# Handing out the first FFN and the preparation of a batch one unit later, and loading x from ScalarE's queue

## Chip, core and metric

The kernel runs on one core of a Trainium2 chip. The metric is the device time of one launch in microseconds, as the median of several runs. A profiled execution of the same program gives the trace and the page from which the lines below come.

The names of the engines are those of the profile: PE is TensorE (matmuls, transposes), PEld its weight loads, DVE is VectorE, ACT is ScalarE, POOL is GpSimd, and SP is SyncE, which does no arithmetic and issues most DMAs. Each engine works through its own instructions in order. An instruction that waits for a semaphore, a DMA issue too, holds everything that stands behind it on its engine.

## What is computed

x has 16 batches of 512 tokens with 128 features. Two layers follow each other. Layer 0, the only one that the change touches, is this:

```python
x = x + 0.5 * _L0_ffn_ref(_layernorm(x), w_gate, w_up, w_down)
x = x + _L0_attn_ref(_layernorm(x), W_qkv, b_qkv, W_out, b_out, rel_emb_k, rel_emb_v)
x = x + 0.5 * _L0_ffn_ref(_layernorm(x), w_gate, w_up, w_down)
```

The FFN quantizes its input, its weights and its hidden values to FP4 in blocks of 16 (`fp4_quant_dequant`) and computes `silu(gate) * up` with 352 hidden values. The attention has 16 heads of 8 features and relative positions, clipped at 64, in both the scores and the values; the softmax runs over all 512 keys of a batch. Layer 1 has another FFN with attention, routing to 8 experts and two layer norms, a linear attention with running sums, and the first part once more.

## The kernel before

Layer 0 is written as steps that Python generators hand out. A **unit** is half a batch: unit u = 2b + h is half h of batch b, so there are 32. The steps of a batch b are:

- `xload(b)` takes one of five buffers of the pool `xk` for the batch's x (128x4x128) and loads it through SP's queue (L475).
- `head(b,h)` runs the first FFN on half h, in place, through `FFN.half` (L107 to L140): layer norm statistics on DVE (L55, L56), normalisation on ACT (L62), quantization on DVE and POOL (L70 to L81), matmuls with a tanh on ACT (L121 to L126), a second quantization, transposes and the last matmul (L133 to L139), and the sum into x on DVE (L140). Its first step calls `xload`.
- `prep(b)` is `Attn0.prep` (L275): layer norm, transposes, q and k, each split into two f16 parts (cast L143 on DVE, difference L144 on POOL). q also goes into the tiles HM (L298). Then DMAs write to DRAM: twelve to QM (L300), three to QS and three to KSd (L302), and four rows to QS (L309). The small parts of these rows are made on DVE (L307, `qkhi` and `qklo`). `qklo` has one buffer, so that each writing of it waits until the DMA that reads the one before is done.
- `loads(u)` reads these back in the order the matmuls need: KS (L315, once per batch), BD (L329) and TQ (L330). KSd, QS and QM have two buffers by batch, BD and TQ three by unit.
- `maxima(u)` computes all 32 score blocks of a unit on PE (L263, and L267 for the relative positions) and takes their maxima on DVE (L341). At its end the negative maxima (`mn`, L352) go to DRAM as MD (L353) and come back as a row of BD (L355), so that the next scores already have the maximum taken off.
- `main(u)` computes the scores again, ACT takes exponentials into PT (L369), and PE multiplies them with the values into `av` and with the relative values into `rps`. `rps` is copied to RV (L403), goes to DRAM as RD (L406) and comes back turned as `cr` (L409); `av` is copied to `cx` (L412).
- `fin(u)` adds the two (L422), divides, multiplies with the output weights and adds to x (L442, L443).
- `tail(u)` runs the second FFN on the half and stores it (L486). When both halves of a batch are stored, its x buffer is free for a batch five later.
- `prepV(b)` makes the values V from the transposed x (L321).

The score tiles `sps` share three PSUM banks between `maxima` and `main`, and all other small results (`mps`) share two.

`interleave` decides in which order the steps are handed out. Every entry has a generator, its number of steps n, and a time from f to t in units; the entry whose next step is due first, at f + (t - f) * done / n, is handed out next. `at(g,n,f,t)` adds u to both times. This order is the priority for the framework's scheduler, which then writes each engine's instructions in the order in which it finds them ready. Before, the due times of a unit u = 2b + h are:

```python
pl,hl=2,3
W=dict(part=0,V=(.6,.7),fin=(.45,.9),prep=(0,.7),tail=1.0,head=(-.1,1))
```

So in unit 2b the preparation of batch b + 2 is due from 0 to 0.7, and in units 2b and 2b + 1 the two halves of the first FFN of batch b + 3, each from -0.1 to 1. The maxima run as one long stream, a unit and a half ahead of `main`; half a unit's maxima into unit u, the loads of u + 1 are handed out. Ahead of the loop stand batches 0 to 2 of the first FFN and the preparation of batches 0 and 1.

Of the kernel before, what the change touches and what calls it, by code (L numbers as in the profile page):

```python
# [141 lines left out]
def f16split(nc, src, hi, lo, eng_lo):  # L142
    nc.vector.tensor_copy(hi,src)  # L143
    eng_lo.tensor_tensor(lo,src,hi,ALU.subtract)  # L144

class Attn0:

    def __init__(a, s, wk, pp, wqkv, bqkv, wout, bout, rek, rev):
# [27 lines left out]
        OFF=a.OFF=168  # L176
        W=EW+32
        ekt=wk.tile([8,129],F32,name="ekt")
        with nc.allow_non_contiguous_dma(reason="small"):
            nc.sync.dma_start(ekt,rek.rearrange("r d -> d r"))  # L180
        nc.vector.tensor_tensor(ekt[:,1:],ekt[:,1:],ekt[:,0:1].to_broadcast([8,128]),ALU.subtract)
        pad=wk.tile([8,W],F32,name="pad")
        lo=OFF+24-64
        nc.vector.memset(pad[:,0:lo+1],0.0)
        nc.vector.tensor_copy(pad[:,lo+1:lo+129],ekt[:,1:129])
        nc.vector.tensor_copy(pad[:,lo+129:],ekt[:,128:129].to_broadcast([8,W-lo-129]))
        ph=wk.tile([8,W],F16,name="ph"); pl=wk.tile([8,W],F16,name="pl")
        f16split(nc,pad,ph,pl,nc.vector)
        padk=dr.tile([24,W],F16,name="padk")
        nc.sync.dma_start(padk[0:8],ph); nc.sync.dma_start(padk[8:16],ph); nc.sync.dma_start(padk[16:24],pl)  # L190
# [255 lines left out]
def interleave(*gens):  # L446

    live=[[g,n,0,f,t] for g,n,f,t in (q if len(q)==4 else (*q,0,1) for q in gens)]
    while live:
        k=min(live,key=lambda r:r[3]+(r[4]-r[3])*r[2]/r[1])  # L450
        try: next(k[0]); k[2]+=1
        except StopIteration: live.remove(k)
# [4 lines left out]
def layer0(tc, s, w, src, dst, nb=16):  # L457
    nc=tc.nc
    tok=lambda x,b: x[b].rearrange("(t p) d -> p t d",p=128)
    P="L0_attn_"; names=["W_qkv","b_qkv","W_out","b_out","rel_emb_k","rel_emb_v"]  # L460
    with ExitStack() as c:
        s.const=c.enter_context(tc.tile_pool(name="c",bufs=1))
        pM=c.enter_context(tc.tile_pool(name="pM",bufs=2,space=PS))
        pF=c.enter_context(tc.tile_pool(name="pF",bufs=0,space=PS)) if 0 else pM
        pS=c.enter_context(tc.tile_pool(name="pS",bufs=3,space=PS))
        pX=pS
        pA=c.enter_context(tc.tile_pool(name="pA",bufs=1,space=PS))
        wk=c.enter_context(tc.tile_pool(name="wk",bufs=1))
        fk=c.enter_context(tc.tile_pool(name="fk",bufs=2))
        xk=c.enter_context(tc.tile_pool(name="xk",bufs=5))  # L470
        X={}
        def xload(b):
            if b in X or b>=nb: return
            t=xk.tile([128,4,128],F32,name="x"); X[b]=t
            nc.sync.dma_start(t,tok(src,b))  # L475
        def head(b,h):

            if b<nb: xload(b); yield from F.half(X[b],h,fk,pF)
        def prep(b):
            if b<nb: yield from A.prep(b,X[b],wk,pM)  # L480
        def prepV(b):
            if b<nb: yield from A.prepV(b,pM)
        def tail(b,h):
            if b<0: return
            yield from F.half(X[b],h,fk,pF)
            nc.sync.dma_start(tok(dst,b)[:,2*h:2*h+2,:],X[b][:,2*h:2*h+2,:])  # L486
        def mxs(b,half):
            if b>=nb: return
            yield from A.maxima(b,half,wk,pX,pM)
        def loads(u):  # L490
            if u<2*nb:
                if u%2==0: A.loadK(u//2)
                A.load(u//2,u%2)
        def stream():
            for u in range(1,2*nb):
                for k,_ in enumerate(mxs(u//2,u%2)):
                    if k==16: loads(u+1)
                    yield
        st=stream()
        def part(n):  # L500
            for _ in range(n):
                if next(st,0)==0: return
                yield
        pl,hl=2,3
        W=dict(part=0,V=(.6,.7),fin=(.45,.9),prep=(0,.7),tail=1.0,head=(-.1,1))
        with tc.tile_pool(name="wp",bufs=1) as wp:
            for b in range(3): xload(b)
            F=FFN(s,w["L0_ffn_w_gate"],w["L0_ffn_w_up"],w["L0_ffn_w_down"],wp,pF)
            ffn2=lambda f,b: interleave((f(b,0),21,0,.8),(f(b,1),21,.2,1))
            ffn2(head,0)  # L510
            A=Attn0(s,wp,pS,*[w[P+n] for n in names])
            def run(g):
                for _ in g: pass
            run(prep(0)); run(prepV(0)); loads(0); run(mxs(0,0))
            FFN1.pre(s,wp,[pA.tile([128,512],F32,name=f"av{z}") for z in range(2)]+[pA.tile([128,512],F32,name="rps")],w)
        big=c.enter_context(tc.tile_pool(name="big",bufs=3))
        loads(1); ffn2(head,1); run(prep(1)); run(part(14)); ffn2(head,2)
        S=[(part(99999),33*2*nb,W['part'],2*nb+W['part'])]
        for b in range(nb):
            for h in range(2):  # L520
                u=2*b+h
                def at(g,n,f,t): S.append((g,n,u+f,u+t))
                at(A.main(b,h,X,wk,big,pS,pA,pM),59,0,1)
                fn,tl=(W['fin'],W['tail']) if u<2*nb-2 else ((.3,.5),.6)
                at(A.fin(b,h,X,wk,pM),5,1+fn[0],1+fn[1])
                at(tail(b,h),21,1+fn[1]+.001,1+fn[1]+tl)
                if b+hl<nb: at(head(b+hl,h),21,*W['head'])
                if h==0 and b+pl<nb: at(prep(b+pl),11,*W['prep'])
                if h==1 and b+1<nb: at(prepV(b+1),1,*W['V'])
        interleave(*S)  # L530
# [251 lines left out]
class Attn1:  # L782
# [38 lines left out]
    X={}  # L821
# [188 lines left out]
def run_stages(ctx, tc, w, out):  # L1010
    s = K(ctx, tc)
    X2 = s.dram.tile([16, 512, 128], F32, name="X2")
    layer0(tc, s, w, w["L0_attn_x"], X2)
    layer1(tc, s, w, X2, out)
# [23 lines left out]
```

## Time and profile before

| what | value |
|---|---|
| median of 3 runs | 3630.38 us (3630.13 to 3631.83) |
| the profiled execution's own time | 3633.94 us |
| its span, first to last instruction | 3632.2 us |
| mean granted TensorE clock | 0.900 of full speed |
| first exponential of unit 0, and of unit 1 | 175.5 us, 237.4 us |
| last exponential of unit 31 ends | 1975.1 us |

A span's busy shares are means over stages that differ: layer 0 takes the first 2045 us or so, layer 1 the rest. Rows of the profile give the line, the engine, the operation, what it writes and reads, how often, and microseconds. A row of waits reads: engine and line, `<-` what released it, microseconds in total, times, longest. Rows of a timeline begin with the start and the duration in microseconds and end, in brackets, with the idle time of the engine before them and what ended it.

### The profile page before, as it was taken

What the parts mean: (1) busy time and instruction counts of PE and PEld (TensorE: products, weight loads), DVE (VectorE), ACT (ScalarE), POOL (GpSimd) and SP (SyncE); (2) the same over time, 40 slices, a digit from 0 to 9 for tenths busy, and PEclk for the clock granted to TensorE, in tenths of its full rate; (3) what the DMA queues carried; (4) which work ended last, traced back from release to release, by engine and by line L of the source; (5) the groups of instructions that cost most, each with busy time, mean ns of one, the idle gap of its engine ahead of it and who ended that gap; (6) DMA issues with size and microseconds to landing.
All of it is one profiled execution on the core that took longest, in us unless ns stands there. A gap on an engine that the chain in (4) does not pass through costs nothing. (4 is left out here: it accounts for less than half of the span.)

```text
span 3632.2 us, 95259 instructions
## 1 busy us (share of the span) xinstructions
PE 2825.0 (78%) x40077; PEld 2032.3 (56%) x40077; DVE 2444.9 (67%) x6508; ACT 1693.8 (47%) x3391; POOL 838.9 (23%) x789
## 2 busy tenths in 40 slices
PE   5578989889898889888896388873788888878570
PEld 3357777667676677666775244431565555555230
DVE  5568788777887788877773467774546655655356
ACT  3145555545455454545554155533455454445242
POOL 4122222222222222222110222212112211111226
PEclk8799999999999999999998599886899989989785
DMA  3232222321223222222210111104312222121401
GB/s 105 54 91 71 57 53 59 81 63 52 65 65 77 64 50 58 76 74 62 53 33 19 32 33 36 36 33 123 90 54 73 59 63 56 36 62 36 126 17 46
DMA packets 290159, 217.23 MB, mean 60 GB/s; under 512 B 77402, under 2 KB 257476, under 8 KB 289604
## 3 DMA queue, kind: packets, MB, share of 16 engines
q1 hardware_dynamic: 284468, 207.72, 21.6%
q8 instruction: 315, 5.16, 0.6%
q10 hardware_dynamic: 5264, 3.43, 0.4%
q14 instruction: 112, 0.92, 0.1%
HBM read 110.28 MB, written 100.78 MB: 58 GB/s over the span
## 5 line engine op out<-in xcount | busy, mean ns | idle before, releaser
L341 DVE TRANSPOSE_TENSOR_REDUCE mx<-sps 128x16 f32<-128x512 f32 x1024 | 702.5, 701 | 261.7 <-PE sps L263 137.2
L263 PE MATMUL sps<-a_BD,a_KS 128*128 128x128 f16 x8192 | 736.4, 222 | 136.2 <-DVE mx L341 65.6
L369 ACT ACTIVATE PT<-sps 128x512 f32<-128x512 f32 x1024 | 576.4, 599 | 433.8 <-PE sps L267 238.1
L263 PEld LDWEIGHTS <-a_KS 128*128 128x128 f16 x8192 | 546.1, 98 | 296.4 <-issue 260.0
L59 POOL TENSOR_TENSOR ln_rs<-ln_ve,negh 128x4 f32<-128x4 f32 (+1 forms) x192 | 176.9, 930 | 855.1 <-DVE ln_ve L58 760.6
L267 PE MATMUL sps<-a_TQ,a_ET 128*128 128x64 f16 x7168 | 370.3, 195 | 0.0
L721 DVE SCALAR_TENSOR_TENSOR moe<-mps,oh,moe 128x128 f32<-128x128 f32 x896 | 289.8, 341 | 110.7 <-PE mps L719 96.5
L79 POOL TENSOR_TENSOR q_M<-q_y,q_M 128x704 f32<-128x704 f32 (+2 forms) x129 | 157.0, 1218 | 784.6 <-DVE q_y L78 658.6
L719 PE MATMUL mps<-f_W,T 128*128 128x512 f32 x512 | 297.1, 701 | 24.8 <-DVE moe L721 20.0
L267 PEld LDWEIGHTS <-a_ET 128*128 128x128 f16 x7168 | 311.2, 99 | 2.3 <-issue 1.9
L274 PE MATMUL av<-PT,a_V 128*32 128x256 f32 x3840 | 251.9, 387 | 0.0
L894 DVE TENSOR_TENSOR a_at<-pp,a_cm 128x1024 f32<-128x1024 f32 x128 | 154.3, 1214 | 79.6 <-PE pp L892 78.6
L892 PE MATMUL pp<-a_F 64*128 64x128 f32 x2048 | 169.8, 306 | 41.4 <-DVE a_at L894 30.2
L892 PEld LDWEIGHTS pp<-a_F 64*128 64x128 f32 x2048 | 143.3, 206 | 93.0 <-DVE a_at L894 36.9
L719 PEld LDWEIGHTS mps<-f_W,T 128*128 128x128 f32 x512 | 102.7, 222 | 125.0 <-issue 75.3
L274 PEld LDWEIGHTS av<-PT,a_V 128*32 128x32 f32 x3840 | 121.4, 111 | 68.7 <-issue 5.0
L874 ACT ACTIVATE a_F<-pp 128x1024 f32<-128x1024 f32 x128 | 127.0, 1025 | 46.8 <-PE pp L872 40.5
L62 ACT ACTIVATE xn<-xn,ln_mr,ln_rs 128x128 f32<-128x128 f32 x256 | 103.6, 481 | 95.5 <-DVE ln_mr L60 75.2
L274 PE MATMUL rps<-PT,a_TV 128*32 128x64 f32 x6912 | 134.5, 222 | 4.6 <-issue 4.4
L139 PE MATMUL mps<-wdT,hT 128*128 128x128 f32 (+1 forms) x768 | 126.9, 301 | 5.6 <-ACT hT L136 4.0
L673 ACT COPY f_PT<-St 32x512 f32<-32x512 f32 x128 | 78.7, 615 | 106.0 <-DVE St L672 99.9
L872 PE MATMUL pp<-a_QK,a_PK 128*128 128x512 f16 x256 | 82.7, 413 | 54.4 <-DMA a_QK<-a1d 26.6
(342 smaller groups left out, 5330.2 us busy)
## 6 DMA issues: line engine op xcount, KB each, us to landing
QM<-a_HM SPq DMA_DIRECT2D x180, 128.0 KB
a_TQ<-QM SPq DMA_DIRECT2D x120, 192.0 KB
RD<-RV SPq DMA_DIRECT2D x32, 512.0 KB
a_KS<-KSd SPq DMA_DIRECT2D x128, 96.0 KB
a_QK<-a1d SPq DMA_DIRECT2D x128, 96.0 KB
xn<-X SPq DMA_DIRECT2D x32, 256.0 KB
a1d<-a_hi SPq DMA_DIRECT2D x64, 128.0 KB
a_BD<-QS SPq DMA_DIRECT2D x128, 58.0 KB
```

What stands on the lines that cost most here:

```text
L59: nc.gpsimd.tensor_tensor(rs,ve,s.negh[:,:n],ALU.pow); yield
L79: nc.gpsimd.tensor_tensor(M[:P],y[:P],M[:P],ALU.subtract)
L263: nc.tensor.matmul(o4[:,g],KS[:,sd,g*512+kt*128:g*512+(kt+1)*128],BD[:,g,:,b*32:b*32+32].rearrange("p h (x j) -> p x h j",j=4),start=(g==0 ...
L267: nc.tensor.matmul(out[:,x*64:x*64+64],a.ET[:,w0:w0+128],TQ[:,:,b*32+4*x:b*32+4*x+4],start=False,stop=(x==7),skip_group_check=True)
L274: for p,q in mms[1:]: a.nc.tensor.matmul(*p,**q)
L341: with a.s.tc.high_priority(): r=nc.vector.tensor_reduce(mx[:,kt,:,bb],ps.rearrange("p (i c) -> p i c",c=32),axis=AX.X,op=ALU.max,apply_tr ...
L369: nc.scalar.activation(pt[:,:,bb*32:bb*32+32].rearrange("p h (x j) -> p x h j",j=4),ps.rearrange("p (x h j) -> p x h j",x=8,j=4),AF.Exp)
L719: nc.tensor.matmul(ps,yT[:,j*128:(j+1)*128],a.W[:,e2*4:e2*4+4,:],start=True,stop=True)
L721: nc.vector.scalar_tensor_tensor(moe[:,j,:],ps[:,e*128:(e+1)*128],oh[:,j,e2*4+e:e2*4+e+1],moe[:,j,:],ALU.mult,ALU.add)
L874: nc.scalar.activation(f,ps,AF.Relu)
L892: nc.tensor.matmul(ps[:,hh,bs],f[hh*64:hh*64+64,1,bs],f[hh*64:hh*64+64,0,bs],start=True,stop=True)
L894: nc.vector.tensor_tensor(k,ps.rearrange("p h (b q) -> p (h b) q",b=4),a.cm.unsqueeze(1).to_broadcast([128,8,128]),ALU.mult)
```

## The change

Three things change in `layer0`; no arithmetic is added or taken away.

- `head` no longer loads x. A step of its own, `xl(b)`, loads it through ACT's queue (`nc.scalar`); it is due in unit 2b of two batches before at -1.4 to -1.3. Batches 0 to 2 are still loaded ahead of everything through SP.
- The first FFN of batch b + 2 (no longer b + 3) is due from -1.05 to 0 of units 2b and 2b + 1. For one batch this is a unit later. As hl is now 2, batch 2 is handed out inside the loop; due times are kept from falling below 0.
- The preparation of batch b + 2 is due from 1.03 to 1.9 of unit 2b, that is in the odd unit that follows.

```diff
-        def xload(b):
-            if b in X or b>=nb: return
+        def xload(b, eng=nc.sync):
             t=xk.tile([128,4,128],F32,name="x"); X[b]=t
-            nc.sync.dma_start(t,tok(src,b))
+            eng.dma_start(t,tok(src,b))
+        def xl(b):
+            xload(b,nc.scalar); yield
         def head(b,h):
 
-            if b<nb: xload(b); yield from F.half(X[b],h,fk,pF)
+            if b<nb: yield from F.half(X[b],h,fk,pF)
...
-        pl,hl=2,3
-        W=dict(part=0,V=(.6,.7),fin=(.45,.9),prep=(0,.7),tail=1.0,head=(-.1,1))
+        pl,hl=2,2
+        W=dict(part=0,V=(.6,.7),fin=(.45,.9),prep=(1.03,1.9),tail=1.0,head=(-1.05,0))
...
-        loads(1); ffn2(head,1); run(prep(1)); run(part(14)); ffn2(head,2)
+        loads(1); ffn2(head,1); run(prep(1)); run(part(14))
...
-                def at(g,n,f,t): S.append((g,n,u+f,u+t))
+                def at(g,n,f,t): S.append((g,n,max(u+f,0),max(u+t,.5)))
...
+                if h==0 and 2<b+hl<nb: at(xl(b+hl),1,-1.4,-1.3)
                 if b+hl<nb: at(head(b+hl,h),21,*W['head'])
```

## The prediction

> **What bounds the kernel now.** The page first: how long, which engines, where.
>
> ```profile
> span 3632.2 us, 95259 instructions
> ...
> PE 2825.0 (78%) x40077; PEld 2032.3 (56%) x40077; DVE 2444.9 (67%) x6508; ACT 1693.8 (47%) x3391; POOL 838.9 (23%) x789
> ...
> PE   5578989889898889888896388873788888878570
> DVE  5568788777887788877773467774546655655356
> ```
>
> Each digit is 90.8 us. The first 22 slices are layer 0, which alone is changed; there PE is at 8 to 9 tenths and DVE at 7 to 8. No engine is full, so I cut the loop into stretches of one batch (two units), from the first exponential of a batch to that of the next; eleven batches follow (span, then busy time by engine).
>
> ```profile
> 886.50:1003.70 117.20, 103.42 (x1827) 81.90 (x1826) 91.80 (x208) 58.89 (x131) 27.64 (x26) 0.97 0.26 64
> ...
> sum 1270.10, PE 1126.32 PEld 889.13 DVE 1013.58 ACT 647.67 POOL 306.91; mean PE 102.39 PEld 80.83 DVE 92.14 ACT 58.88 POOL 27.90
> ```
>
> A batch takes 115.5 us, of which PE works 102.4. The other 13.1 us are what an order of instructions can win or lose. The list of waits between 400 and 1600 us says who holds whom (sum, times, longest):
>
> ```profile
> PE sps L263 <- DVE mx L341: 41.7, 42, 3.9
> ...
> DVE ln_st L55 <- DMA x<-in_L_attn_x_dram: 45.5, 11, 5.2
> DVE qklo L307 <- DMA KSd<-qklo: 3.9, 4, 1.3
> ...
> SPq L475 <- DMA X<-x: 28.8, 11, 3.4
> SPq L355 <- DMA MD<-mn: 72.4, 21, 4.4
> ```
>
> PE's largest wait is for the maxima on DVE, and DVE's largest wait that is not for PE is for a batch's x: 4.1 us, once per batch. The timelines of SP, DVE and PE show one:
>
> ```profile
> 873.37 0.39 SPq L486 DMA_DIRECT2D X<-x  x1
> 876.73 0.39 SPq L475 DMA_DIRECT2D x<-in_L_attn_x_dram  x1
> 879.93 1.07 DVE L55 BATCH_NORM_STATS2 ln_st<-x 128x6 f32<-128x128 f32 x5 [4.11 <-DMA x<-in_L_attn_x_dram]
> 882.54 0.39 PE L263 MATMUL sps<-a_BD,a_KS 128*128 128x128 f16 x4 [2.85 <-DVE mx L341]
> ```
>
> The x buffer is free only when an old batch's result has been stored; SP waits for that (2.97 us after the store's issue), loads x, and DVE, in order, stands at the first statistics. PE goes on for a while, then stands too.
>
> **Part 1, the load of x.** In eleven stretches, each from the start of such a wait to 5 us after it, 100.5 us in all, PE worked 65.9 and was idle 34.6. Outside them it is idle (143.8 - 34.6) / (1270.1 - 100.5) = 9.3%, which would be 9.4 us. So the waits cost PE 25.2 us, 2.3 each; the first 4.1 - 2.3 = 1.8 us of such a wait are absorbed. In the changed program's order the load stands on ACT after the third exponential of an even unit, and its first reader on DVE after the fourth of the next unit's maxima, which begin in the trace over half a unit, some 30 us, later. The wait goes: **-25 us** (bounds -45, all of DVE's time, and -15).
>
> The wait for the store does not go; it moves to ACT. ACT reaches the load some 3.5 us after the unit's first exponential (six take 5.0 us at 886.51, a hT pair 0.6). The store stands on SP behind RD, three KS and two BD loads: by their rows 0.6 + 1.2 + 1.2 us, then 0.4 to 3.5 us for the store and 3.0 to its landing. RD starts about 2 us before the unit, so the load is free at +4.4 to +7.5: a wait of 1 to 4 us, with exponentials queued behind it, and behind these PE for want of a free sps bank. I take 2 us, absorbed like the first 1.8 above: **0** (bounds 0 and 11 x 2.2 = +24). The issue, 0.39 us on SP, lies in ACT's idle half.
>
> [...]
>
> **Part 2, the preparation a unit later.** No instruction is added, but its 12 QM, 6 QS/KSd and 4 row writes now stand elsewhere in SP's queue. Today:
>
> ```profile
> 1024.75 1.23 SPq L302 DMA_DIRECT2D QS<-qkhi  x2
> 1026.62 8.65 SPq L300 DMA_DIRECT2D QM<-a_HM  x12
> ...
> 1036.03 1.43 SPq L302 DMA_DIRECT2D KSd<-qkhi  x2
> ...
> 1039.74 0.53 SPq L302 DMA_DIRECT2D KSd<-qklo  x1
> ...
> 1040.98 1.28 SPq L353 DMA_DIRECT2D MD<-mn  x2
> ...
> 1047.17 2.50 SPq L355 DMA_DIRECT2D a_BD<-MD  x4
> ...
> 1024.30 0.43 DVE L143 CAST qkhi<-qk 128x512 f16<-128x512 f32 x1 [1.42 <-ACT qk L291]
> ...
> 1042.13 0.68 DVE L307 TENSOR_TENSOR qklo<-mps,qkhi 32x512 f16<-32x512 f32 x1 [1.33 <-DMA KSd<-qklo]
> ```
>
> L307 writes the one buffer qklo, so DVE must wait until the DMA KSd<-qklo has read it. Counted from the end of the cast L143, over the eleven batches from 443 to 1601 us, SP has issued that DMA at 13.8 to 15.5 us (mean 14.5), it lands 1.85 us later, and DVE, which gets there after eight maxima, waits 0.5 to 1.7 us. The maxima's exchange (MD, then BD) comes after it.
>
> In the changed order that exchange stands in the middle of the QM writes, ahead of KSd<-qklo: 1.3 us for MD, 4.9 us until BD may start (1042.26 to 1047.17), 2.5 us for BD, less two QM writes of 0.6 issued meanwhile: 7.5 us. On long batches SP also waited 1.6 us for POOL there, which the earlier QS<-qklo removes; I take 7.0. So the DMA is issued at 21.5 us and lands at 23.4. DVE again has eight maxima between, and 40 instructions instead of 28, many of 0.1 to 0.3 us: 15.6 us without today's wait, plus some 2. It waits 5.5 us (bounds: 1, as now, and 7.5). Behind L307 stand all later maxima, so PE; 1.8 us are absorbed: 3.7 us x 13 batches = **+48 us** (bounds 0 and 13 x 5.7 = +74).
>
> The 4.9 us decide this. [...]
>
> **Part 3, the rest.** At the start, preparation of batch 2 ran today into four BD loads that held SP 7.7 us:
>
> ```profile
> 253.19 0.68 DVE L307 CAST qkhi<-mps 32x512 f16<-32x512 f32 x1 [8.43 <-DMA QS<-qkhi]
> ```
>
> and PE then stood 9.0 us; unit 1 took 68.5 us instead of 58. Half a unit later these loads are through: **-9 us** (bounds -9, 0). ACT's copies into RV wait 13.6 us in 400 to 1600 for RD to land; RD now goes ahead of the TQ loads: **-2** (bounds -5, 0). One head half leaves the first units and lies in unit 26, and preparation in unit 27, which takes 48.6 us today against 58: the work is moved, **0** (bounds -6, +8). The TQ loads (3.5 us each when they queue) still end about 7 us before the maxima that read them: 0. Layer 1 has the same instructions, slightly reordered by the scheduler: 0 (bounds -4, +4).
>
> Sum: -25 + 0 + 48 - 9 - 2 = +12 us on the profiled execution's 3633.9 us, which is 3646; that execution is 3.6 us above the runs' median of 3630.4, so about **3642 us**.
>
> **Rivals.** *DVE comes later to L307 (faster).* If its 40 instructions take as long as KSd<-qklo does, nothing replaces the wait for x. For: the scheduler chose this place with its own idea of the landing. Against: today, too, that idea was 1 us short, with the exchange not yet in the path. Price: -25 - 9 - 2 = -36, so 3594; with DVE's full 45 us, 3574. The point is a wait of (36 / 13) + 1.8 = 4.6 us at L307: below it the change gains.
>
> *ACT becomes the bound (slower).* If the store's issue is held up (3.3 us at 945.25, behind two BD loads, as it will stand now) and SP comes late to RD because KS waits for KSd, the load of x may hold ACT 6 to 8 us: 11 x (4 to 6) = 45 to 65 us more, 3687 to 3707. Against: SP has the end of the odd unit to catch up in.
>
> *Nothing moves.* Both waits are of like size, 4.1 and 4.6 us, and PE's 102.4 us stay: 3630. So too if the load, which leaves only when the store has landed, is not really earlier.
>
> **Numbers.** Forecast 0.47 (3634 to 3670), faster rival 0.30 (3580 to 3620), ACT 0.13 (3670 to 3710), nothing 0.10 (3624 to 3637). A measurement of this kernel tells 0.2%, 7 us, from no change. Faster: the first rival and a little of the forecast, 0.31. Same: the last rival and the forecast's lower edge, 0.14. Slower: 0.55. The range takes in most of both sides, 3596 to 3690; the forecast's own is 3634 to 3670.
>
> **What would show it.** In the changed profile DVE's wait for x is gone from the list, DVE qklo L307 <- DMA KSd<-qklo has about 5 us a batch, unit 1 is near 58 us, and ACT shows some 2 us before the load of x. If L307 waits under 2 us, or units are under 57 us, I am wrong towards faster; if ACT's exponentials stand over 5 us each batch behind that load, towards slower.

## The result, and the profile after

The changed kernel takes 3755.67 us (median of four runs, 3748.60 to 3773.11) against 3630.26 us: 1.0356 of the kernel before, 95% interval 1.0315 to 1.0397, some 125 us slower. The forecast was 3642 us. Slower was right, the size was not: about 110 us are missing, and they lie in one term, which was put at 0.

Page of the changed kernel: engines, PE by slices, and the two groups at PE and ACT whose idle time grew.

```profile
span 3771.4 us, 95337 instructions
...
PE 2855.7 (76%) x40077; PEld 2067.5 (55%) x40077; DVE 2455.8 (65%) x6508; ACT 1696.5 (45%) x3391; POOL 833.8 (22%) x789
...
PE   5588779777977887787889548883588888888570
...
L263 PE MATMUL sps<-a_BD,a_KS 128*128 128x128 f16 x8192 | 753.2, 224 | 270.3 <-ACT PT L369 156.3
...
L369 ACT ACTIVATE PT<-sps 128x512 f32<-128x512 f32 x1024 | 574.2, 599 | 660.0 <-PE sps L263 280.2
```

The same two groups in the kernel before:

```profile
L263 PE MATMUL sps<-a_BD,a_KS 128*128 128x128 f16 x8192 | 736.4, 222 | 136.2 <-DVE mx L341 65.6
L369 ACT ACTIVATE PT<-sps 128x512 f32<-128x512 f32 x1024 | 576.4, 599 | 433.8 <-PE sps L267 238.1
```

In layer 0 (the first 22 slices, of 94.3 us here) PE is mostly at 7 to 8 tenths where it was at 8 to 9. Its idle time ahead of the scores is 270.3 us where it was 136.2, and what ends most of it is now ACT, no longer DVE's maxima. Layer 1 has not moved: from the end of layer 0's last exponential to the span's end it is 1661 us, before 1657, and 1650 to 1670 in every kernel below.

The list of waits, 400 to 1600 us:

```profile
PE sps L263 <- ACT PT L369: 129.6, 50, 12.7
...
ACT PT L369 <- DMA a_BD<-QS: 65.1, 5, 14.0
ACT PT L369 <- DMA X<-x: 64.2, 5, 14.2
...
DVE qklo L307 <- DMA KSd<-qklo: 46.5, 10, 5.6
...
PE sps L263 <- DVE mx L341: 42.7, 72, 1.4
```

DVE's wait for x is gone and its wait at L307 is there with 4.7 us a batch, both as forecast. New are the two rows of ACT: exponentials that waited for a DMA, 12.9 us each time, once a batch. An exponential reads nothing that a DMA writes; what waited is the load of x just ahead of it, and the names are the profile's inference from times (e9 has what the load waits on). One such place, on SP, ACT and PE:

```profile
1180.07 0.54 SPq L406 DMA_DIRECT2D RD<-RV  x1
1180.66 4.02 SPq L315 DMA_DIRECT2D a_KS<-KSd  x3
1184.79 4.53 SPq L329 DMA_DIRECT2D a_BD<-QS  x2
1189.41 2.95 SPq L487 DMA_DIRECT2D X<-x  x1
```

```profile
1184.91 0.60 ACT L369 ACTIVATE PT<-sps 128x512 f32<-128x512 f32 x1 [0.27 <-PE sps L267]
1197.53 0.37 ACTq L474 DMA_DIRECT2D x<-in_L_attn_x_dram  x1
1197.95 1.09 ACT L369 ACTIVATE PT<-sps 128x512 f32<-128x512 f32 x2 [12.44 <-DMA a_BD<-QS]
```

```profile
1187.34 0.30 PE L115 MATMUL mps<-ident,q_M 128*128 128x128 f32 x1
1198.60 0.59 PE L263 MATMUL sps<-a_BD,a_KS 128*128 128x128 f16 x4 [10.96 <-ACT PT L369]
```

ACT comes to the load at 1185.51, after three exponentials. At that time SP still stands in the KS and BD loads; the store of the old batch is issued only at 1189.41 to 1192.36, and the load leaves 5.2 us later. PE fills the sps banks that are left and then does nothing for 11 us. The even units of these batches last 67 to 70 us, where they lasted 56 to 58.

### The profile page after: what moved, and what is told of

It is laid out like the page before. It is cut to its first block, busy times and chain, and to the rows that moved or that the text cites. A ratio compares the mean times of both kernels' runs of the same rounds, so it can differ in the third digit from the quotient of the medians.

```text
span 3771.4 us, 95337 instructions
## 1 busy us (share of the span) xinstructions
PE 2855.7 (76%) x40077; PEld 2067.5 (55%) x40077; DVE 2455.8 (65%) x6508; ACT 1696.5 (45%) x3391; POOL 833.8 (22%) x789
## 5 line engine op out<-in xcount | busy, mean ns | idle before, releaser
L263 PE MATMUL sps<-a_BD,a_KS 128*128 128x128 f16 x8192 | 753.2, 224 | 270.3 <-ACT PT L369 156.3
L263 PEld LDWEIGHTS <-a_KS 128*128 128x128 f16 x8192 | 558.9, 100 | 439.4 <-issue 402.0
L876 ACT ACTIVATE a_F<-pp 128x1024 f32<-128x1024 f32 x128 | 126.6, 1026 | 46.0 <-PE pp L874 39.7
L133 PE MATMUL mps<-ident,q_M 128*128 128x128 f32 (+1 forms) x384 | 72.3, 313 | 87.9 <-DVE qklo L307 51.9
L139 PE MATMUL mps<-wdT,hT 128*128 128x128 f32 (+1 forms) x768 | 128.4, 307 | 6.4 <-ACT hT L136 5.5
L121 PE MATMUL mps<-wguT,f_x 128*128 128x352 f32 x256 | 120.6, 558 | 14.6 <-ACT f_x L116 13.7
```

What stands on the lines that cost most here:

```text
L139: nc.tensor.matmul(ps[:,384:512],hT[:P,c,:],f.wdT[:P,c,:],start=(c==0),stop=(c==2),skip_group_check=True)
L263: nc.tensor.matmul(o4[:,g],KS[:,sd,g*512+kt*128:g*512+(kt+1)*128],BD[:,g,:,b*32:b*32+32].rearrange("p h (x j) -> p x h j",j=4),start=(g==0 ...
```

## The experiments

Theory T: the loss is ACT's wait at the load (12.9 us a batch; the expectations have 12.6, without the load's own issue of 0.4) and DVE's wait at L307, less what the load gained. Rival R: the later hand-out itself crowds the units. Rival Q, added after the first runs: ScalarE's queue is itself the cost. Each kernel was timed beside the kernel before on the same chip; ratios are to that (median 3630.26 us for the changed kernel, 3645.47 for e1 to e4, 3640.30 for e5 to e8, 3644.90 for e9 to e11). "Batch" is the mean of eleven batches (first exponential of unit 4 to that of unit 26); the waits are means of the 10 to 12 that the lists of waits have between 400 and 1700 us, at the load of x, at L307 and at the first statistics of x; PE busy and granted clock are means of the windows of these batches.

| kernel | median us | ratio (95%) | batch us | at load | L307 | x | PE busy, clock |
|---|---|---|---|---|---|---|---|
| before | 3630.26 | 1 | 115.5 | 0 | 0.9 | 4.1 | 102.4, 0.98 |
| changed | 3755.67 | 1.0356 (1.0315 to 1.0397) | 128.4 | 12.9 ACT | 4.6 | 0 | 104.3, 0.92 |
| e1 | 3781.51 | 1.0370 (1.0336 to 1.0403) | 128.5 | 12.7 POOL | 4.8 | 0 | 106.1, 0.91 |
| e2 | 3647.55 | 1.0003 (0.9988 to 1.0019) | 116.0 | 0 | 5.2 | 0 | 102.9, 0.96 |
| e3 | 3694.96 | 1.0126 (1.0091 to 1.0160) | 120.9 | 0 | 4.1 | 3.0 | 102.9, 0.97 |
| e4 | 3720.98 | 1.0209 (1.0175 to 1.0243) | 121.4 | 14.1 ACT | 0 | 0 | 102.1, 0.95 |
| e5 | 3651.65 | 1.0033 (1.0013 to 1.0053) | 116.0 | 0 | 5.1 | 0 | 102.9, 0.96 |
| e6 | 3762.66 | 1.0335 (1.0300 to 1.0370) | 126.6 | 11.9 ACT | 4.7 | 0 | 104.5, 0.93 |
| e7 | 3564.62 | 0.9789 (0.9755 to 0.9823) | 109.7 | 0 | 0 | 0 | 100.5, 0.99 |
| e8 | 3624.48 | 0.9958 (0.9938 to 0.9978) | 114.9 | 0 | 0 | 4.2 | 102.1, 0.98 |
| e9 | 3714.42 | 1.0195 (1.0163 to 1.0228) | 121.2 | 5.1 ACT | 4.8 | 0 | 104.8, 0.95 |
| e10 | 3639.22 | 0.9996 (0.9978 to 1.0015) | 115.7 | 0 | 5.2 | 0 | 102.9, 0.97 |
| e11 | 3587.40 | 0.9862 (0.9820 to 0.9904) | 110.1 | 0 | 0 | 0 | 101.3, 0.99 |

Below, a ratio is turned into microseconds by 3630.

**e1: the load on GpSimd's queue.**

```diff
-            xload(b,nc.scalar); yield
+            xload(b,nc.gpsimd); yield
```

> The changed kernel, only the load of x issued on GpSimd's queue in place of ScalarE's. Theory T (the changed kernel loses about 109 us because ScalarE stands 11 times 12.6 us at the load of x, with exponentials queued behind it, and about 45 us at L307): GpSimd stands in ScalarE's place, nothing of the attention is queued behind it for long, so some 80 to 109 us come back: 3640 to 3675 us, the waits of ACT for X<-x and a_BD<-QS are gone from the list, DVE qklo L307 <- KSd<-qklo keeps 4 to 6 us a batch. Theory R (the later first FFN and preparation themselves crowd the units, and ScalarE's wait only shows time that something else would have taken): over 3715 us, PE waiting for DVE or for ACT's other work in place of the load.

T's number is missed by some 90 us, R's is met, and yet R is not what the trace shows. The list of waits and a piece of POOL's and of PE's timeline:

```profile
POOL x L474 <- DMA X<-x: 127.1, 10, 14.8
...
PE mps L115 <- POOL q_M L81: 97.9, 10, 12.1
```

```profile
1196.91 0.83 POOL L474 DMA_DIRECT2D x<-in_L_attn_x_dram  x1 [12.37 <-DMA X<-x]
1197.77 0.74 POOL L79 TENSOR_TENSOR q_M<-q_y,q_M 128x256 f32<-128x256 f32 x1
1198.58 0.62 POOL L81 TENSOR_TENSOR q_M<-q_M,xq_sc 128x256 f32<-128x256 f32 x1
```

```profile
1199.26 0.69 PE L115 MATMUL mps<-ident,q_M 128*128 128x128 f32 x2 [9.45 <-POOL q_M L81]
```

ACT no longer waits. But on POOL the quantization of the first FFN is queued behind the load, PE's transposes of its result (L115) stand in PE's order ahead of the next scores, and so PE is idle for 9.8 us a batch all the same. What failed was the step "nothing of the attention is queued behind it": POOL is only 22% busy, but one of its results stood next.

**e2: the load on SyncE's queue, at its new place in the program.**

```diff
-            xload(b,nc.scalar); yield
+            xload(b,nc.sync); yield
```

> The changed kernel, only the load of x back on SyncE's queue, at its new place. T: ScalarE's wait goes (-109 us), but SP now stands 3 to 5 us for the store in each batch, and the exchange of the maxima and the QM writes behind it come later: 3650 to 3690 us, SPq L476 (x) <- DMA X<-x 11 times 3 us. R: over 3715 us.

The time is that of the kernel before, some 20 us under T's 3650 to 3690. SP does not stand at all:

```profile
1114.95 2.95 SPq L487 DMA_DIRECT2D X<-x  x1
...
1124.82 3.58 SPq L330 DMA_DIRECT2D a_TQ<-QM  x1
1128.45 0.74 SPq L474 DMA_DIRECT2D x<-in_L_attn_x_dram  x1
1145.01 1.29 SPq L353 DMA_DIRECT2D MD<-mn  x2
```

On SP the scheduler put the load behind the TQ loads, 10.6 us after the store's issue ends, and SP's next work comes 16 us later. The new hand-out is therefore not what costs 125 us: R falls. The whole difference between this kernel and the changed one, 128 us, hangs on where the load of x waits.

**e3: only the preparation a unit later.**

```diff
-        W=dict(part=0,V=(.6,.7),fin=(.45,.9),prep=(0,.7),tail=1.0,head=(-.1,1))
+        W=dict(part=0,V=(.6,.7),fin=(.45,.9),prep=(1.03,1.9),tail=1.0,head=(-.1,1))
```

> The kernel before, only the preparation handed out a unit later; first FFN, load of x and its queue as before. T: the wait of DVE at L307 for KSd<-qklo appears, 4 to 6 us a batch, and costs about 45 us: 3660 to 3690 us; DVE's wait for x (4 us a batch) stays. If L307's wait costs PE little: 3620 to 3640 us. R: 3700 us or more, PE waiting for other things than L307.

46 us more than the kernel before. Its list of waits has both of DVE's waits:

```profile
DVE qklo L307 <- DMA KSd<-qklo: 41.2, 10, 4.9
...
DVE ln_st L55 <- DMA x<-in_L_attn_x_dram: 32.5, 11, 6.0
```

The two lists account for only part of it. L307's wait is 3.2 us a batch longer than before and x's 1.1 us shorter, yet a batch is 5.4 us longer. Some 3 us a batch stay unexplained; PE has more of the shorter waits for DVE than before. An earlier start (unit 4 begins 6 us sooner) and a shorter end (9 us, layer 1's spread in it) take some 15 us back.

**e4: rlo gets room of its own, L307's wait is taken out of the changed kernel.**

```diff
-        rhi=wk.tile([128,512],F16,name="qkhi",bufs=2)[:32]; rlo=wk.tile([128,512],F16,name="qklo")[:32]
+        rr=wk.tile([128,512],F16,name="qkhi",bufs=2); rhi=rr[:32]; rlo=rr[32:64]
```

> The changed kernel, only rlo written into partitions 32 to 63 of the buffer of rhi, so that L307 needn't wait until KSd<-qklo has read qklo. T: DVE's wait at L307 is gone or under 1 us, ScalarE's 12.6 us at the load of x stay: 35 to 50 us less than the changed kernel, 3705 to 3720 us. R: within 10 us of the changed kernel, the wait at L307 replaced by another one of DVE or PE.

53 us less than the changed kernel, and no wait at L307. What ACT waits for at the load has other names now:

```profile
ACT PT L369 <- DMA a_TQ<-QM: 98.8, 7, 15.1
...
ACT PT L369 <- DMA X<-x: 56.6, 4, 15.1
```

The load of x neither reads nor writes TQ, and in the program's list it waits for no TQ load: it waits for the old batch's stores and a KS load, as e9 explains. The name is inferred from times.

**e5: the load on ScalarE's queue, 13 instructions later.** The due time does not decide this place: with -1.2 or -1.15 for -1.4 the order of the instructions is the same. The load has to be tied to an exponential.

```diff
...
+                if kt==1 and bb==3: a.lx=r.ins if hasattr(r,"ins") else r
...
-            xload(b,nc.scalar); yield
+            with s.tc.issue_after(A.lx): xload(b,nc.scalar)
+            yield
```

> The changed kernel, the load of x still on ScalarE's queue, only 13 instructions later there (behind the twelfth exponential of the even unit), some 12 us. Theory T (it is the place in an in-order queue that costs, 12.6 us before the store has landed, and the price falls on whatever engine stands there): the wait of ACT for X<-x shrinks to 0 to 3 us a batch and no DVE wait for x comes, since its first reader is 30 us on; 90 to 110 us less than the changed kernel, within 20 us of the kernel before. Theory Q (ScalarE's queue is itself the cost, or its DMA starts late): at least 60 us of the 125 stay.

```profile
1120.69 0.60 ACT L369 ACTIVATE PT<-sps 128x512 f32<-128x512 f32 x1 [0.47 <-PE sps L267]
1120.83 0.37 ACTq L475 DMA_DIRECT2D x<-in_L_attn_x_dram  x1
1121.25 0.60 ACT L369 ACTIVATE PT<-sps 128x512 f32<-128x512 f32 x1
```

No wait before the load here, nor in five more of the eleven batches; in the other five it is 0.4 to 1.9 us. 117 us of the 129 are gone. Q falls: where the store has already landed, the same queue gives 116.0 us a batch, as SP's does in e2.

**e6: a sixth buffer for x.** To make room, the quantization writes q_y over f_h.

```diff
-        y=wk.tile([128,max(704,n)],F32,name=("q_y","q_yw")[n>704])[:,:n]; y3=...
+        y=X if n==704 else wk.tile([128,max(352,n)],F32,name=("q_y","q_yw")[n>704])[:,:n]; y3=...
...
-        xk=c.enter_context(tc.tile_pool(name="xk",bufs=5))
+        xk=c.enter_context(tc.tile_pool(name="xk",bufs=6))
```

> The changed kernel with a sixth buffer for x, so that the load, at its early place on ScalarE's queue, waits for a store issued a batch earlier; room is made by writing q_y over f_h, in place. T: ACT's wait at the load is gone, 90 to 115 us less than the changed kernel, within 20 us of the kernel before; L307 keeps its 4 to 6 us. Q: the load's issue holds ACT although no store is waited for, and at least 60 of the 125 us stay.

A miss: 11.9 us a batch remain, and the time. In the order of ACT's instructions the load of batch 6 now stands where that of batch 5 stood. The scheduler puts a load as early as it believes the buffer to be free, and with six buffers that is right behind the store of the same old batch 0. The experiment took nothing away.

**e9: the sixth buffer, with the load held at its place** behind the third exponential (e5's tie with kt==0, bb==2, and e6's edits).

> The changed kernel with the sixth x buffer (q_y written over f_h for room) and the load of x tied behind the third exponential of the even unit, where it stood in the changed kernel. In e6 the scheduler had moved each load a whole batch earlier, behind the store of the same old batch, so that nothing was taken away; here the store was issued a batch, some 115 us, earlier. Theory T (ACT is held by the landing of the store): the wait of ACT is gone, 95 to 125 us less than the changed kernel, within 20 us of the kernel before. Theory Q (issuing at that place in the queue is what holds ACT): at least 60 of the 125 us stay.

Half a miss: 5.1 us of ACT's 12.9 remain, and 58 us are gone, where T wanted 95 at least. The store was issued a batch earlier, so it is not the store that is waited for:

```profile
PE sps L263 <- ACT PT L369: 57.5, 57, 4.8
ACT PT L369 <- DMA a_KS<-KSd: 56.3, 11, 6.3
```

The programs' lists of instructions say what a load waits on, here that of the changed kernel and of e9:

```
L474 DMACopy x_8457<-in_L0_attn_x_dram 128x4x128 [waits DMAHW3_49,DMAHW7_49,DMAHW2_49,DVE_49]
L475 DMACopy x_10588<-in_L0_attn_x_dram 128x4x128 [waits DMAHW6_49,DMAHW3_49,DMAHW2_49]
```

The programs know eight such semaphores, DMAHW0 to DMAHW7, and every DMA of SP and ACT (1669 and 36 in the changed kernel) adds to one of them when it lands. Counted through the lists, two of the three belong to the two stores of the old batch. The third is the one to which the load itself adds, and its last user before the load is in each of these batches, in both kernels, a KS load of SP, which lands 9 to 11 us after its issue. In e9 the semaphores of the stores are complete before ACT comes to the load, and that of the KS load completes just before the load leaves, eleven times of eleven. In the changed kernel it is the other way round: the KS load's semaphore is complete 5 to 8 us before the load leaves (1190.93 us at the place above) and the store's just before (1197.43). So there ACT's wait ends with the store; but had the store been early, the shared semaphore would still have held ACT for some 5 us. An experiment that takes away the sharing alone was not run.

**e7: both costs out, e2 and e4 together.**

> The changed kernel with both costs taken out: the load of x at its new place on SyncE's queue (e2) and rlo in the buffer of rhi (e4). T: the two add, so e2's time, equal to the kernel before, less 40 to 50 us: 0.986 to 0.990 of the kernel before, the fastest so far. If the wait at L307 was only where DVE's slack showed, another wait takes its place: over 0.995.

0.9789, better than expected and the fastest of all: 77 us less than the kernel before. The windows of e2 and of e7, sums over eleven batches (the first number is the time, then busy time by engine):

```profile
sum 1275.80, PE 1131.79 PEld 902.76 DVE 1023.27 ACT 646.56 POOL 300.37; mean PE 102.89 PEld 82.07 DVE 93.02 ACT 58.78 POOL 27.31
```

```profile
sum 1206.40, PE 1105.62 PEld 878.53 DVE 1014.25 ACT 647.94 POOL 300.32; mean PE 100.51 PEld 79.87 DVE 92.20 ACT 58.90 POOL 27.30
```

A batch is 6.3 us shorter though the wait at L307 was 5.2 us; PE does the same matmuls in 2.4 us less, at a clock of 0.99 where it was 0.96.

**e8: e4's edit in the kernel before.**

> The kernel before with rlo in the buffer of rhi, nothing else: what that edit is worth by itself. T: L307 waits 0.5 to 1.7 us a batch there and 8.4 us once at the start, so 0 to 15 us less than the kernel before (0.996 to 1.0); 0.99 or less would mean that e4 and e7 owe their gain to something else than the wait that the later preparation makes.

15 us less, the most that was expected, and small beside the 53 us of e4 and the 78 of e7 against e2, which take the same wait out where it is 5 us long.

**e10: e6's edits in the kernel before.**

> The kernel before with a sixth x buffer (q_y written over f_h for room), nothing of the change: what DVE's wait for x is worth by itself. If 1.8 us of each wait are absorbed, as the prediction reckoned: 20 to 30 us less than the kernel before. If nothing is absorbed, and PE's granted clock rises with it (as the 4.9 us a batch between e3 and e2 suggest): 45 to 60 us less, 0.983 to 0.988.

No change, a miss. DVE's wait for x is gone from the list, but this has come:

```profile
PE mps L430 <- DVE qklo L307: 60.3, 11, 7.7
DVE qklo L307 <- DMA KSd<-qklo: 56.7, 11, 7.3
```

**e11: e10 and e8 together.**

> The kernel before with a sixth x buffer and rlo in the buffer of rhi: both waits taken out without the change. If the waits add: e10's gain and e8's 15 us, 0.979 to 0.985 of the kernel before, and so the same as e7. If the later units of the change are worth something of their own, e7 stays faster by over 15 us.

0.9862. The sixth buffer (with q_y written over f_h, which was not run by itself) is worth nothing alone and 35 us once L307 is free. In e10 one wait took the other's place, and not only because DVE comes sooner: SP issues KSd<-qklo 25.9 us after the cast L143 on the average, 14.5 us before, since the cast now falls while SP still stands for RD to land (at 1123 us). e7 remains 27 us faster by the ratios, with intervals that meet at 0.982. In the profiles it is 23 us. Layer 0's last exponential ends 10 us earlier in e7, because its unit 4 starts 13 us earlier (408.1 against 421.1). The other 13 us lie behind it (1653 us against 1666, in the spread of 1650 to 1670 above), where the change touches nothing. So what the later units are worth of their own is shown for 10 us at most.

## Why the prediction was wrong, point by point

**Part 1, the load of x.** That DVE's wait goes was right. Its worth, -25, was low but inside its bounds: 45 us between e3 and e2 (which also moves the first FFN), 35 between e8 and e11, and nothing in e10, where another wait took its place.

**The wait for the store on ACT is the step that failed: 0, with bounds 0 and +24; it measured 117 (e5) to 128 us (e2).** The wait was put at 2 us, all of it absorbed; it was 12.9 us a batch. Three things were wrong. First, the sizes of the chain on SP. Three KS loads, and two BD loads, were taken at 1.2 us each from rows of the old order; in the new one, behind the preparation's writes and five other KS loads, they hold SP for 4.02 and 4.53 us. The store took 2.95, in the range given, and from there to the load it was 5.2 us, not 3.0. RD to load is 17.5 us where 6.4 to 9.5 was reckoned. Second, a wait that was not in the sum: the semaphore shared with a KS load. In the changed kernel it lies inside the wait for the store and adds nothing; e9 shows the 5.1 us that it holds ACT when the store is early. Third, "absorbed". The table gives little sign of it: with no waits a batch takes 109.7 us (e7), and most kernels lie above that by the sum of their waits and some 1 us more, 5.2 us of wait giving 6.3 (e2), 9.9 giving 11.5 (e9), 17.5 giving 18.7 (changed). Only e4, with 11.7 for 14.1, absorbs some; e3, with 11.2 for 7.1, loses more than its waits. PE's idle time within 5 us of a wait, from which the 1.8 us came, missed what was lost later.

That the kernel got slower at all was forecast from the other terms, and there it was luck: without ACT's wait the change moves nothing (e2, 1.0003, interval 0.9988 to 1.0019), where the sum had +12. All of the loss came with the term that was put at 0.

The rival "ACT becomes the bound" had the right object and half of the mechanism: the store is held up behind two BD loads, but RD is not late (it starts 2.3 us before the unit at the place above, about 2 forecast). It had 6 to 8 us for a wait of 12.9, less absorption; its 45 to 65 us are half of what was measured, and its chance of 0.13 was too small. The argument against it, that SP catches up in the odd unit, does not hold in the SP rows above: SP issues RD in time and still brings the store 9.3 us later.

**Part 2, the preparation a unit later,** held in its mechanism. The exchange of the maxima stands in the middle of the QM writes, ahead of KSd<-qklo:

```profile
1155.85 0.55 SPq L300 DMA_DIRECT2D QM<-a_HM  x1
1157.02 1.28 SPq L353 DMA_DIRECT2D MD<-mn  x2
1158.35 1.26 SPq L300 DMA_DIRECT2D QM<-a_HM  x2
1163.29 2.44 SPq L355 DMA_DIRECT2D a_BD<-MD  x4
1165.78 7.04 SPq L300 DMA_DIRECT2D QM<-a_HM  x9
...
1174.20 0.56 SPq L302 DMA_DIRECT2D KSd<-qklo  x1
```

KSd<-qklo is issued 20.6 us after the cast on the average (21.5 forecast), and the wait is 4.6 us for 5.5 (the prediction's own terms, 23.4 less 17.6, give 5.8). From the end of MD's issue to BD's it is 5.0 us here, as in the trace from which the forecast took 4.9. The rival in which DVE comes later to L307 falls. The size is less certain. +48 was forecast, and only this edit gives +46 (e3), but of that the waits explain part, and it contains the earlier start, which the prediction counted in Part 3. Taking the wait out gives 53 us in the changed kernel (e4) and, where ACT does not stand, 78 (e7 against e2).

**Part 3.** Unit 1 is 56.0 us (forecast 58) and unit 4 begins 11 us sooner, 411.1 us for 422.3; ACT's wait for RD is gone, layer 1 is where it was. In e7 against e11 the earlier start is still there.

The measured steps add up: +46 from the kernel before to e3, -45 from e3 to e2, +128 from e2 to the changed kernel, together the 129 us that the ratio 1.0356 gives. The earlier start is inside them. As they are differences between neighbours, they must add up, and this is no further test.

Which engine issues the load made no difference to a batch in these runs: at the early place ACT and POOL give 128.4 and 128.5 us (changed, e1), at a late one ACT and SP both give 116.0 (e5, e2).

## What to carry to other kernels

In the runs here a DMA issue that had to wait held its engine like any other instruction that waits: ACT for 12.9 us a batch (changed), POOL for 12.7 (e1), as DVE stood 4.6 us at L307. Put it on a queue where it comes after the event it waits for, and not on an engine because that engine is idle on average; what counts is the next instruction behind it and who waits for that. Price such a wait from the rows of its issuer in the new order, with the transfers that will stand before it, and count it in full unless a run shows that some of it is absorbed. An edit that removes one wait (e10) may show nothing, because it lets another take its place, until that one is removed too (e11).

## What the runs showed of the hardware

Behind ACT's wait at the load the trace shows a second thing, a lower granted clock on PE. The windows around the wait of the changed kernel shown above (columns as before, then granted clock, DMA share and GB/s):

```profile
1177.00:1187.00 10.00, 9.64 (x158) 9.29 (x159) 8.44 (x24) 3.28 (x9) 2.28 (x4) 0.83 0.52 128
1187.70:1198.50 10.80, 0.00 (x0) 0.00 (x0) 0.47 (x3) 0.55 (x2) 0.00 (x0) 0.65 0.26 73
1198.50:1202.00 3.50, 3.40 (x27) 2.96 (x27) 0.72 (x1) 2.48 (x6) 0.00 (x0) 0.50 0.54 142
1202.00:1206.00 4.00, 4.00 (x54) 2.77 (x52) 1.24 (x2) 0.80 (x2) 0.00 (x0) 0.68 0.22 62
1206.00:1210.00 4.00, 4.00 (x54) 2.94 (x47) 2.85 (x5) 2.25 (x5) 0.00 (x0) 1.00 0.06 12
```

After 10.8 us of rest PE runs at half clock although it is busy for 3.40 of the next 3.50 us and all of the 4.00 after them; cut finer, the same trace has 0.50 up to 1204.5 us and 1.00 from 1205, some 6 us after PE resumed; four matmuls of L263 take 0.59 us there (1198.60 us) and 0.39 us before (1184.25 us). Over a batch PE is busy for 104.3 us at a mean clock of 0.92 in the changed kernel and for 102.9 at 0.96 in e2. The busy time does not follow the clock alone: e4 has 102.1 us at 0.95. Where L307 waits 5 us a batch the mean clock is lower too (0.96 in e2, 0.99 without these waits in e7).

The other surprise was what an issue can cost on SP. In the changed kernel, 400 to 1700 us, the issue of one KS load took 0.3 to 2.2 us and that of one BD load from QS 0.2 to 6.4. It is not enough that the preparation's writes stand ahead: three KS loads right behind them took 1.14 us at 1176.62, and three more, after two others, QS writes and RD, 4.02 us at 1180.66. So the store was late before it was issued. What the long issues waited for, the runs don't show.
